# Two transposes taken off TensorE: blocks exchanged by DMA, turned on VectorE

## The chip, the cores and the metric

One core of one Trainium2 chip. The metric is the device time of one execution in microseconds (us), the median of several runs. The kernel before takes 2883.35 us (4 runs, 2882.38 to 2884.21).

## The reference

128 samples of 128 tokens by 512 features, all fp32. Each sample goes through two layers that share one 128x128 adjacency matrix; samples do not depend on each other.

```python
# x: (128, 128, 512), adj: (128, 128); layernorm without affine part, eps 1e-5
h = maximum(layernorm(x), 0)                       # layer 0: graph convolution
x = x + einsum('nm,bmd->bnd', adj, h) @ weight + bias
h = maximum(layernorm(x), 0)                       # layer 1: masked attention, 8 heads of 64
q, k, v = split(h @ w_qkv)
a = softmax(where(adj == 0, -inf, q @ k.T * 64**-0.5))
o = (a @ v) @ w_proj + b_proj
x = x + o + layernorm(o) * ln_gamma + ln_beta
```

## The kernel before

It is a software pipeline over the samples: one turn of the loop works on one sample in each of some twenty stages, and several samples are under way at once. The order of the calls in the loop is the order in which each engine gets its instructions, and the traces show each engine working in that order.

Two operands are transposed before TensorE uses them; as the kernel calls these products, both operands have the axis summed over on the partitions: the normed layer-1 input `h1` (tokens by features becomes features by tokens), and the attention probabilities (8 heads of 128x128). Before, TensorE does it by products with an identity matrix (0.43 and 0.87 us a sample, from the starts in its timeline), and ScalarE copies the results out of PSUM, where the kernel puts them (an evacuation; one of 585 ns and two of 592 ns a sample, medians of L172 and L232).

```python
def norm1_out(i):
    H1[i] = work.tile([P, D], F32, name="h1")
    relu_norm(H1[i], X1[i], *ST1.pop(i))                      # VectorE: shift; ScalarE: relu
    nc.gpsimd.tensor_tensor(X1[i], X1[i], beta_b, op=ALU.add)

def flip(i):                                                   # h1 -> h1T
    ...
    p = mm_psum("pflip")
    for c in range(C):
        nc.tensor.transpose(p[:, c * P:(c + 1) * P], H1[i][:, c * P:(c + 1) * P], ident)
    nc.scalar.copy(H1T[g][:, :, j, :], p.rearrange("p (c n) -> p c n", c=C))
    ...
def softmax_divide(i):
    ...
    nc.gpsimd.tensor_tensor(s, s, sm.unsqueeze(2).to_broadcast([P, H, P]), op=ALU.mult)

def flip_probs(i):                                             # probabilities -> pT
    PT[i] = work.tile([P, 2 * C, P], F32, name="pT")
    for e in range(2):
        p = psum.tile([P, C, P], F32, tag="at", name=f"pp{e}")
        for c in range(C):
            nc.tensor.transpose(p[:, c, :], S[i][:, e * C + c, :], ident)
        nc.scalar.copy(PT[i][:, e * C:(e + 1) * C, :], p)
    ...
for i in range(2 - LOAD, B + 1):
    at(load, i + LOAD - 1)            # nc.sync.dma_start, one DMA of 256 KB (conditions of the first turns cut)
    at(scores, i)
    at(norm1_out, i + 8)
    at(softmax_shift, i)
    at(qk, i + G, 0)
    at(flip_probs, i - 1)
    at(softmax_exp, i)
    at(norm0, i + 11)
    at(qk, i + G, 1)
    at(softmax_divide, i)
    at(norm0_out, i + 11)
    at(attend, i - 1)
    at(values, i + 4)
    at(mix, i + 10)
    at(project, i - 1)
    at(flip, i + 8)
    at(finish, i - 1)                 # ends with nc.sync.dma_start of the result, 256 KB
    at(layer0, i + 9)
```

Only two DMAs a sample leave from the sync queue (SP): the load and the store.

Of the kernel before, what the change touches and what calls it, by code (L numbers as in the profile page):

```python
# [8 lines left out]
F32 = mybir.dt.float32  # L9
AF = mybir.ActivationFunctionType  # L10
ALU = mybir.AluOpType
AX = mybir.AxisListType

P = 128
# [5 lines left out]
def kernel(  # L20
# [22 lines left out]



    nc = tc.nc
    B, N, D = x.shape
    H = 8
    HD = D // H
    C = D // P  # L50
    G = 4
    assert N == P and HD * 2 == P and B % G == 0
    scale = HD ** -0.5

    const = ctx.enter_context(tc.tile_pool(name="const", bufs=1))
    work = ctx.enter_context(tc.tile_pool(name="work", bufs=2))
    stat = ctx.enter_context(tc.tile_pool(name="stat", bufs=4))
    psum = ctx.enter_context(tc.tile_pool(name="psum", bufs=4, space=bass.MemoryType.PSUM))
    ctx.enter_context(tc.manual_schedule())

    X, H0, YT, X1, H1, H1T, QKT, V, S, PT, OT, O, ST0, ST1, STO = ({} for _ in range(15))

    def mm_psum(name):
        return psum.tile([P, 512], F32, tag="mm", name=name)

    def load(i):
        X[i] = work.tile([P, D], F32, name="x", bufs=6)
        nc.sync.dma_start(out=X[i], in_=x[i])

    LOAD = 14  # L70
    for i in range(2):
        load(i)


    ident = const.tile([P, P], F32)
# [16 lines left out]
    def load_layer1():  # L92
        nc.sync.dma_start(out=wqkv_sb, in_=w_qkv.rearrange("(c p) o -> p c o", p=P))
        nc.sync.dma_start(out=wp_sb, in_=w_proj.rearrange("(c p) o -> p c o", p=P))
        for t, src in ((bp_b, b_proj), (gamma_b, gamma), (beta_b, beta)):
            nc.sync.dma_start(out=t, in_=src.partition_broadcast(P))
# [18 lines left out]
    def stats_of(src):  # L115

        st = stat.tile([P, nc.vector.BN_STATS_DIM], F32, name="st")
        nc.vector.bn_stats(st, src)  # L118
        mv = stat.tile([P, nc.vector.BN_AGGR_DIM], F32, name="mv")
        nc.vector.bn_aggr(mv, st)  # L120
        ve = stat.tile([P, 1], F32, name="ve")
        nc.vector.tensor_scalar(ve, mv[:, 1:2], EPS, None, op0=ALU.add)  # L122
        rs = stat.tile([P, 1], F32, name="rs")
        nc.gpsimd.tensor_tensor(rs, ve, minus_half, op=ALU.pow)  # L124
        return mv[:, 0:1], rs

    def relu_norm(dst, src, mean, rs):
        shift = stat.tile([P, 1], F32, name="shift")
        nc.vector.tensor_scalar(shift, mean, rs, -1.0, op0=ALU.mult, op1=ALU.mult)  # L129
        nc.scalar.activation(dst, src, AF.Relu, bias=shift, scale=rs)  # L130
# [6 lines left out]
    def norm0_out(i):  # L137
        relu_norm(H0[i], X[i], *ST0.pop(i))
        nc.gpsimd.tensor_tensor(X[i], X[i], b0_b, op=ALU.add)
# [10 lines left out]
    def layer0(i):  # L150
        p = mm_psum("pl0")
        for c in range(C):
            nc.tensor.matmul(p, lhsT=YT[i][:, c, :], rhs=w0_sb[:, c, :], start=(c == 0), stop=(c == C - 1))  # L153
        X1[i] = work.tile([P, D], F32, name="x1", bufs=12)
        nc.vector.tensor_tensor(X1[i], p, X[i], op=ALU.add)
        ST1[i] = stats_of(X1[i])
        del X[i], YT[i]

    def norm1_out(i):
        H1[i] = work.tile([P, D], F32, name="h1")  # L160
        relu_norm(H1[i], X1[i], *ST1.pop(i))
        nc.gpsimd.tensor_tensor(X1[i], X1[i], beta_b, op=ALU.add)  # L162


    def flip(i):
        g, j = divmod(i, G)
        if j == 0:
            H1T[g] = work.tile([P, C, G, P], F32, name="h1T")
        p = mm_psum("pflip")
        for c in range(C):  # L170
            nc.tensor.transpose(p[:, c * P:(c + 1) * P], H1[i][:, c * P:(c + 1) * P], ident)  # L171
        nc.scalar.copy(H1T[g][:, :, j, :], p.rearrange("p (c n) -> p c n", c=C))  # L172
        del H1[i]

    def qk(i, k):

        g, m = i // G, 2 * (i % G) + k
        if m == 0:
            QKT[g] = work.tile([P, 2 * C, G, P], F32, name="qkT")
        p = mm_psum("pqk")  # L180
# [6 lines left out]
    def values(i):  # L187
        g, j = divmod(i, G)
        p = mm_psum("pv")
        for c in range(C):  # L190
            nc.tensor.matmul(p, lhsT=H1T[g][:, c, j, :], rhs=wqkv_sb[:, c, 2 * D:], start=(c == 0),  # L191
                             stop=(c == C - 1))
        V[i] = work.tile([P, D], F32, name="v", bufs=7)
        nc.scalar.copy(V[i], p)

    def scores(i):

        g, j = divmod(i, G)
        ps = [psum.tile([P, C, P], F32, tag="at", name=f"ps{e}") for e in range(2)]
        for c in range(C):  # L200
            for e in range(2):
                r = slice(e * HD, (e + 1) * HD)
                nc.tensor.matmul(ps[e][:, c, :], lhsT=QKT[g][r, c, j, :], rhs=QKT[g][r, C + c, j, :],  # L203
                                 start=True, stop=True)
        s = S[i] = work.tile([P, 2 * C, P], F32, name="s")
        m4 = maskb.unsqueeze(1).to_broadcast([P, C, P])
        for e in range(2):
            nc.vector.tensor_tensor(s[:, e * C:(e + 1) * C, :], ps[e], m4, op=ALU.add)
# [10 lines left out]
    def softmax_divide(i):  # L219
        s = S[i]  # L220
        sm = stat.tile([P, H], F32, name="sm")
        nc.vector.tensor_reduce(sm, s, AX.X, ALU.add)  # L222
        nc.vector.reciprocal(sm, sm)
        nc.gpsimd.tensor_tensor(s, s, sm.unsqueeze(2).to_broadcast([P, H, P]), op=ALU.mult)  # L224

    def flip_probs(i):
        PT[i] = work.tile([P, 2 * C, P], F32, name="pT")
        for e in range(2):
            p = psum.tile([P, C, P], F32, tag="at", name=f"pp{e}")
            for c in range(C):  # L230
                nc.tensor.transpose(p[:, c, :], S[i][:, e * C + c, :], ident)  # L231
            nc.scalar.copy(PT[i][:, e * C:(e + 1) * C, :], p)  # L232
        del S[i]

    def attend(i):
        p = psum.tile([P, C, P], F32, tag="at", name="po")
# [18 lines left out]
    def finish(i):  # L255
        o = O.pop(i)
        mean, rs = STO.pop(i)
        t = work.tile([P, D], F32, name="t", bufs=3)
        nc.vector.scalar_tensor_tensor(t, o, mean, gamma_b, op0=ALU.subtract, op1=ALU.mult)  # L259
        nc.gpsimd.tensor_tensor(o, o, X1[i], op=ALU.add)  # L260
        nc.vector.scalar_tensor_tensor(t, t, rs, o, op0=ALU.mult, op1=ALU.add)  # L261
        nc.sync.dma_start(out=out[i], in_=t)
        del X1[i]

    def at(f, i, *a):
        if 0 <= i < B:
            f(i, *a)



    for i in range(2 - LOAD, B + 1):
        if i > 2 - LOAD:
            at(load, i + LOAD - 1)
        if i == 4 - LOAD:
            load_layer1()
        at(scores, i)
        at(norm1_out, i + 8)
        at(softmax_shift, i)
        at(qk, i + G, 0)
        at(flip_probs, i - 1)  # L280
        at(softmax_exp, i)
        at(norm0, i + 11)
        at(qk, i + G, 1)
        at(softmax_divide, i)
        at(norm0_out, i + 11)
        at(attend, i - 1)
        at(values, i + 4)
        at(mix, i + 10)
        at(project, i - 1)
        at(flip, i + 8)  # L290
        at(finish, i - 1)
        at(layer0, i + 9)

# [28 lines left out]
```

## Time and profile before

| | before |
|---|---|
| median, us | 2883.35 |
| TensorE (PE) busy | 98% of the span, 97% of the chain that ended last |
| mean steady period of one sample, us | 21.89 |
| DMAs a sample on the sync queue | 2 |
| time that the sync queue waited for data to store | 2643.6 us |

The mean period is taken from the first and the last evacuation of the attention output (`oT`) between 200 and 2500 us, divided by the samples between them; the same rule is used for every kernel. The last row of the table is this one, from the waits of the sync queue of the kernel before (who waited, for what, us in total, times, longest):

```profile
SPq L262 <- DVE t L261: 2643.6, 128, 38.1
```

### The profile page before, as it was taken

What the parts mean: (1) busy time and instruction counts of PE and PEld (TensorE: products, weight loads), DVE (VectorE), ACT (ScalarE), POOL (GpSimd) and SP (SyncE); (2) the same over time, 40 slices, a digit from 0 to 9 for tenths busy, and PEclk for the clock granted to TensorE, in tenths of its full rate; (3) what the DMA queues carried; (4) which work ended last, traced back from release to release, by engine and by line L of the source; (5) the groups of instructions that cost most, each with busy time, mean ns of one, the idle gap of its engine ahead of it and who ended that gap; (6) DMA issues with size and microseconds to landing.
All of it is one profiled execution on the core that took longest, in us unless ns stands there. A gap on an engine that the chain in (4) does not pass through costs nothing.

```text
span 2880.8 us, 30548 instructions
## 1 busy us (share of the span) xinstructions
PE 2825.2 (98%) x11777; PEld 1465.4 (51%) x11777; DVE 1498.2 (52%) x2695; ACT 886.5 (31%) x1410; POOL 992.0 (34%) x902
## 2 busy tenths in 40 slices
PE   7999999999999999999999999999999999999995
PEld 3555555555555555555555555555555555555543
DVE  3355545555554555555455555555545555554544
ACT  2332332333333233233323323332332333233221
POOL 3233333333333333333333333333333333333222
PEclk9999999999999999999999999999999999999997
DMA  3000000000000000000000000000000000000000
GB/s 132 12 22 30 23 23 23 30 23 22 30 23 22 24 28 22 23 30 23 22 26 26 22 22 30 22 23 30 23 23 23 30 23 23 28 25 15 15 15 18
DMA packets 39313, 75.42 MB, mean 26 GB/s; under 512 B 4224, under 2 KB 4352, under 8 KB 39168
## 3 DMA queue, kind: packets, MB, share of 16 engines
q1 hardware_dynamic: 39168, 73.48, 7.9%
q8 instruction: 92, 1.51, 0.2%
q14 instruction: 53, 0.43, 0.1%
HBM read 39.91 MB, written 33.55 MB: 26 GB/s over the span
## 4 chain that ended last, share of the span: by engine, by line
PE 97%; DVE 1%; POOL 0%; issue 0%; ACT 0%; DMA 0%; POOLq 0%; SPq 0%; ACTq 0%
PE pqk L182 31%; PE pv L191 16%; PE pp L249 16%; PE pl L153 15%; PE ps L203 5%; PE po L240 4%; PE pmix L144 4%; PE pp L231 4%; PE pflip L171 2%; DVE st L118 0%; POOL rs L124 0%; POOL o L260 0%; DVE s L214 0%; ACT h L130 0%; DVE mx L213 0%
## 5 line engine op out<-in xcount | busy, mean ns | idle before, releaser
L182 PE MATMUL pqk<-h1T,wqkv_sb 128*128 128x512 f32 x2048 | 933.1, 599 | 0.0
L124 POOL TENSOR_TENSOR rs<-ve,minus_half 128x1 f32<-128x1 f32 x384 | 258.6, 674 | 1462.6 <-DVE ve L122 1462.2
L251 DVE TENSOR_TENSOR o<-pp,bp_b 128x512 f32<-128x512 f32 x128 | 88.5, 692 | 1003.5 <-PE pp L249 1003.5
L182 PEld LDWEIGHTS pqk<-h1T,wqkv_sb 128*128 128x128 f32 x2048 | 369.3, 190 | 386.7 <-issue 371.6
L130 ACT ACTIVATE h<-x,shift,rs 128x512 f32<-128x512 f32 x256 | 208.4, 814 | 951.2 <-DVE shift L129 951.2
L249 PE MATMUL pp<-wp_sb,oT 128*128 128x512 f32 x1024 | 472.5, 605 | 26.1 <-ACT oT L243 26.1
L191 PE MATMUL pv<-wqkv_sb,h1T 128*128 128x512 f32 x1024 | 473.1, 605 | 0.0
L153 PE MATMUL pl<-w_sb,yT 128*128 128x512 f32 x1024 | 466.5, 599 | 0.0
L224 POOL TENSOR_TENSOR s<-s,sm 128x1024 f32<-128x1024 f32 x128 | 242.7, 1896 | 194.2 <-DVE shift L129 124.3
L249 PEld LDWEIGHTS pp<-wp_sb,oT 128*128 128x128 f32 x1024 | 189.4, 195 | 220.5 <-issue 193.2
L191 PEld LDWEIGHTS pv<-wqkv_sb,h1T 128*128 128x128 f32 x1024 | 184.4, 189 | 207.2 <-issue 207.2
L153 PEld LDWEIGHTS pl<-w_sb,yT 128*128 128x128 f32 x1024 | 186.8, 192 | 187.5 <-issue 187.5
L214 DVE TENSOR_TENSOR s<-s,mx 128x1024 f32<-128x1024 f32 x128 | 257.0, 2008 | 4.4
L162 POOL TENSOR_TENSOR x<-x,beta_b 128x512 f32<-128x512 f32 x128 | 176.2, 1376 | 208.4 <-ACT h L130 204.3
L261 DVE SCALAR_TENSOR_TENSOR t<-t,rs,o 128x512 f32<-128x512 f32 x128 | 96.2, 751 | 213.8 <-POOL o L260 213.8
L172 ACT COPY h1T<-pflip 128x512 f32<-128x512 f32 x128 | 74.9, 585 | 384.8 <-PE pflip L171 384.8
L185 ACT COPY qkT<-pqk 128x512 f32<-128x512 f32 x256 | 147.3, 575 | 114.3 <-PE pqk L182 114.3
L118 DVE BATCH_NORM_STATS2 st<-x 128x6 f32<-128x512 f32 x256 | 176.2, 688 | 5.1 <-DMA x<-in_x_dram 0.7
L217 ACT ACTIVATE s<-s 128x1024 f32<-128x1024 f32 x128 | 135.6, 1059 | 140.0 <-DVE s L214 140.0
L203 PEld LDWEIGHTS ps<-qkT 64*128 64x128 f32 x2048 | 124.2, 187 | 96.7 <-issue 96.7
L222 DVE TENSOR_REDUCE sm<-s 128x8 f32<-128x1024 f32 x128 | 156.2, 1220 | 27.7 <-ACT s L217 15.8
L144 PEld LDWEIGHTS pmix<-adjT,h 128*128 128x128 f32 x1024 | 135.8, 194 | 65.7 <-issue 59.6
(40 smaller groups left out, 2411.0 us busy)
## 6 DMA issues: line engine op xcount, KB each, us to landing
x<-in_x_dram SPq DMA_DIRECT2D x128, 256.0 KB, 2.7
out_dram<-t SPq DMA_DIRECT2D x128, 256.0 KB, 2.0
wqkv_sb<-in_L_gnn_w_qkv_dram SPq DMA_DIRECT2D x1, 3072.0 KB, 15.3
w_sb<-in_L_gnn_weight_dram SPq DMA_DIRECT2D x1, 1024.0 KB, 7.9
wp_sb<-in_L_gnn_w_proj_dram SPq DMA_DIRECT2D x1, 1024.0 KB, 17.5
b_b<-in_L_gnn_bias_dram SPq DMA_DIRECT2D x1, 256.0 KB, 5.4
bp_b<-in_L_gnn_b_proj_dram SPq DMA_DIRECT2D x1, 256.0 KB, 16.2
gamma_b<-in_L_gnn_ln_gamma_dram SPq DMA_DIRECT2D x1, 256.0 KB, 14.8
```

The source lines that it names most:

```text
L118: nc.vector.bn_stats(st, src)
L124: nc.gpsimd.tensor_tensor(rs, ve, minus_half, op=ALU.pow)
L130: nc.scalar.activation(dst, src, AF.Relu, bias=shift, scale=rs)
L144: nc.tensor.matmul(p[:, c * P:(c + 1) * P], lhsT=H0[i][:, c * P:(c + 1) * P], rhs=adjT, start=True, stop=True)
L153: nc.tensor.matmul(p, lhsT=YT[i][:, c, :], rhs=w0_sb[:, c, :], start=(c == 0), stop=(c == C - 1))
L162: nc.gpsimd.tensor_tensor(X1[i], X1[i], beta_b, op=ALU.add)
L182: nc.tensor.matmul(p, lhsT=wqkv_sb[:, c, m * P:(m + 1) * P], rhs=H1T[g][:, c, :, :].rearrange("p b n -> p (b n)"), start=(c == 0), stop=(c ...
L191: nc.tensor.matmul(p, lhsT=H1T[g][:, c, j, :], rhs=wqkv_sb[:, c, 2 * D:], start=(c == 0), stop=(c == C - 1))
L203: nc.tensor.matmul(ps[e][:, c, :], lhsT=QKT[g][r, c, j, :], rhs=QKT[g][r, C + c, j, :], start=True, stop=True)
L214: nc.vector.tensor_tensor(s, s, mx.unsqueeze(2).to_broadcast([P, H, P]), op=ALU.subtract)
L224: nc.gpsimd.tensor_tensor(s, s, sm.unsqueeze(2).to_broadcast([P, H, P]), op=ALU.mult)
L249: nc.tensor.matmul(p, lhsT=OT[i][:, c, :], rhs=wp_sb[:, c, :], start=(c == 0), stop=(c == C - 1))
```

## The change

The intent is to take both transposes off TensorE. A 128x128 transpose is cut in 32x32 blocks. Sixteen DMAs, all between on-chip tiles, bring block (n, q) to the place of block (q, n); one VectorE instruction then turns each block in itself (0.71 us for `h1`, 1.24 us for the probabilities in the run after, whose result is correct). Two such exchanges a sample make 32 DMAs on the sync queue, beside the load and the store.

```diff
-        X[i] = work.tile([P, D], F32, name="x", bufs=6)
+        X[i] = work.tile([P, D], F32, name="x", bufs=5)
...
+    def exchange(dst, src):
+        for n in range(Q):                                   # Q, R = 4, 32
+            for q in range(Q):
+                nc.sync.dma_start(out=dst[q * R:(q + 1) * R, n, :], in_=src[n * R:(n + 1) * R, q, :])
...  (norm1_out)
-        H1[i] = work.tile([P, D], F32, name="h1")
-        relu_norm(H1[i], X1[i], *ST1.pop(i))
+        h1 = work.tile([P, Q, C, R], F32, name="h1")
+        relu_norm(h1.rearrange("p q c r -> p c q r"), X1[i].rearrange("p (c q r) -> p c q r", c=C, q=Q),
+                  *ST1.pop(i))
+        H1[i] = work.tile([P, Q, C * R], F32, name="h1x")
+        exchange(H1[i], h1.rearrange("p q c r -> p q (c r)"))
...  (flip)
-        p = mm_psum("pflip")
-        for c in range(C):
-            nc.tensor.transpose(p[:, c * P:(c + 1) * P], H1[i][:, c * P:(c + 1) * P], ident)
-        nc.scalar.copy(H1T[g][:, :, j, :], p.rearrange("p (c n) -> p c n", c=C))
+        nc.vector.transpose(H1T[g][:, :, j, :].rearrange("p c (q r) -> p q c r", q=Q),
+                            H1.pop(i).rearrange("p q (c r) -> p q c r", c=C))
...  (softmax_divide)
-        nc.gpsimd.tensor_tensor(s, s, sm.unsqueeze(2).to_broadcast([P, H, P]), op=ALU.mult)
+        sq = work.tile([P, Q, H, R], F32, name="sq", bufs=1)
+        nc.gpsimd.tensor_tensor(sq, s.rearrange("p h (q r) -> p q h r", q=Q),
+                                sm.unsqueeze(1).unsqueeze(3).to_broadcast([P, Q, H, R]), op=ALU.mult)
+        S[i] = work.tile([P, Q, H * R], F32, name="sx")
+        exchange(S[i], sq.rearrange("p q h r -> p q (h r)"))
...  (flip_probs)
-        for e in range(2):
-            ...                                              # 4 transposes and one copy each
+        nc.vector.transpose(PT[i].rearrange("p h (q r) -> p q h r", q=Q),
+                            S.pop(i).rearrange("p q (h r) -> p q h r", h=H))
...  (loop)
     for i in range(2 - LOAD, B + 1):
+        at(norm1_out, i + 8)
...
-        at(norm1_out, i + 8)
...
-        at(qk, i + G, 1)
+        at(mix, i + 10)
         at(softmax_divide, i)
         at(norm0_out, i + 11)
+        at(qk, i + G, 1)
         at(attend, i - 1)
         at(values, i + 4)
-        at(mix, i + 10)
+        at(flip, i + 8)
         at(project, i - 1)
-        at(flip, i + 8)
         at(finish, i - 1)
```

Cut: smaller buffer counts for `x1`, `s` and `t`, which make room for the new tiles.

More of the change, by code (lines that the diff above doesn't have):

```diff
@@ L51 @@
     G = 4
+    Q, R = 4, 32
     assert N == P and HD * 2 == P and B % G == 0
@@ L153, in layer0 @@
             nc.tensor.matmul(p, lhsT=YT[i][:, c, :], rhs=w0_sb[:, c, :], start=(c == 0), stop=(c == C - 1))
-        X1[i] = work.tile([P, D], F32, name="x1", bufs=12)
+        X1[i] = work.tile([P, D], F32, name="x1", bufs=11)
         nc.vector.tensor_tensor(X1[i], p, X[i], op=ALU.add)
@@ L168, in flip @@
             H1T[g] = work.tile([P, C, G, P], F32, name="h1T")
-        p = mm_psum("pflip")
-        for c in range(C):
-            nc.tensor.transpose(p[:, c * P:(c + 1) * P], H1[i][:, c * P:(c + 1) * P], ident)
-        nc.scalar.copy(H1T[g][:, :, j, :], p.rearrange("p (c n) -> p c n", c=C))
-        del H1[i]
+        nc.vector.transpose(H1T[g][:, :, j, :].rearrange("p c (q r) -> p q c r", q=Q),
+                            H1.pop(i).rearrange("p q (c r) -> p q c r", c=C))
     def qk(i, k):
@@ L204, in scores @@
                                  start=True, stop=True)
-        s = S[i] = work.tile([P, 2 * C, P], F32, name="s")
+        s = S[i] = work.tile([P, 2 * C, P], F32, name="s", bufs=1)
         m4 = maskb.unsqueeze(1).to_broadcast([P, C, P])
@@ L223, in softmax_divide @@
         nc.vector.reciprocal(sm, sm)
-        nc.gpsimd.tensor_tensor(s, s, sm.unsqueeze(2).to_broadcast([P, H, P]), op=ALU.mult)
+        sq = work.tile([P, Q, H, R], F32, name="sq", bufs=1)
[3 more added lines that the diff above has]
+        exchange(S[i], sq.rearrange("p q h r -> p q (h r)"))
     def flip_probs(i):
         PT[i] = work.tile([P, 2 * C, P], F32, name="pT")
-        for e in range(2):
-            p = psum.tile([P, C, P], F32, tag="at", name=f"pp{e}")
-            for c in range(C):
-                nc.tensor.transpose(p[:, c, :], S[i][:, e * C + c, :], ident)
-            nc.scalar.copy(PT[i][:, e * C:(e + 1) * C, :], p)
-        del S[i]
+        nc.vector.transpose(PT[i].rearrange("p h (q r) -> p q h r", q=Q),
+                            S.pop(i).rearrange("p q (h r) -> p q h r", h=H))
     def attend(i):
@@ L257, in finish @@
         mean, rs = STO.pop(i)
-        t = work.tile([P, D], F32, name="t", bufs=3)
+        t = work.tile([P, D], F32, name="t", bufs=2)
         nc.vector.scalar_tensor_tensor(t, o, mean, gamma_b, op0=ALU.subtract, op1=ALU.mult)
```

## The prediction

> **What bounds the kernel now.** I read the page's busy shares first, then the chain that ended last, then the groups of instructions with shapes kept apart, and last the timeline of single engines in one steady period.
>
> Busy shares and chain, from the page:
> ```profile
> PE 2825.2 (98%) x11777; PEld 1465.4 (51%) x11777; DVE 1498.2 (52%) x2695; ACT 886.5 (31%) x1410; POOL 992.0 (34%) x902
> PE 97%; DVE 1%; POOL 0%; issue 0%; ACT 0%; DMA 0%; POOLq 0%; SPq 0%; ACTq 0%
> PE pqk L182 31%; PE pv L191 16%; PE pp L249 16%; PE pl L153 15%; PE ps L203 5%; PE po L240 4%; PE pmix L144 4%; PE pp L231 4%; PE pflip L171 2%; DVE st L118 0%; POOL rs L124 0%; POOL o L260 0%; DVE s L214 0%; ACT h L130 0%; DVE mx L213 0%
> ```
> TensorE is the bound, 97% of the chain. The lines to be removed are the transposes, L231 (4%) and L171 (2%).
>
> One steady period on TensorE, from its timeline (start, duration, instruction):
> ```profile
> 2008.74 0.60 PE L171 MATMUL pflip<-ident,h 128*128 128x128 f32 x4
> 2009.17 3.60 PE L153 MATMUL pl<-w_sb,yT 128*128 128x512 f32 x8
> 2012.70 1.16 PE L203 MATMUL ps<-qkT 64*128 64x128 f32 x16
> 2013.79 3.70 PE L182 MATMUL pqk<-h1T,wqkv_sb 128*128 128x512 f32 x8
> 2017.33 1.04 PE L231 MATMUL pp<-ident,s 128*128 128x128 f32 x8
> 2018.20 3.60 PE L182 MATMUL pqk<-h1T,wqkv_sb 128*128 128x512 f32 x8
> 2021.73 1.09 PE L240 MATMUL po<-pT,v 128*64 128x128 f32 x16
> ...
> 2030.62 0.60 PE L171 MATMUL pflip<-ident,h 128*128 128x128 f32 x4
> ```
> From start to start there is no gap: the period is 2030.62 - 2008.74 = 21.88 us a sample. Ends overlap, so I cost by differences of starts: pflip takes 9.17 - 8.74 = 0.43 us, the eight probability transposes 18.20 - 17.33 = 0.87 us.
>
> VectorE in the same period:
> ```profile
> 2008.94 0.69 DVE L251 TENSOR_TENSOR o<-pp,bp_b 128x512 f32<-128x512 f32 x1 [7.93 <-PE pp L249]
> ...
> 2015.42 0.15 DVE L122 TENSOR_SCALAR ve<-mv 128x1 f32<-128x1 f32 x1
> 2015.50 1.28 DVE L208 TENSOR_TENSOR s<-ps,maskb 128x512 f32<-128x512 f32 x2
> 2016.69 0.20 DVE L129 TENSOR_SCALAR shift<-mv,rs 128x1 f32<-128x1 f32 x1
> 2016.81 1.22 DVE L213 TENSOR_REDUCE mx<-s 128x8 f32<-128x1024 f32 x1
> 2018.06 2.17 DVE L214 TENSOR_TENSOR s<-s,mx 128x1024 f32<-128x1024 f32 x1
> ```
> VectorE waits 7.93 us for the projection and then works without much pause until after the softmax. That the engine is 52% busy hides that its work lies in one burst right after the projection; a thing added to the burst can reach TensorE.
>
> DMA issue, from the queue's timeline and the DMA view:
> ```profile
> 1.65 0.42 SPq L81 DMA_DIRECT2D adj_sb<-in_adj_dram  x1
> 2.12 0.43 SPq L83 DMA_DIRECT2D b_b<-in_L_gnn_bias_dram  x1
> 2.59 0.43 SPq L85 DMA_DIRECT2D w_sb<-in_L_gnn_weight_dram  x1
> out_dram<-t SPq DMA_DIRECT2D x128, 256.0 KB, 2.0
> ```
> A free queue issues one DMA per 0.47 us whether it holds 64 KB or 1 MB; 256 KB lands 2.0 us after issue.
>
> [...] The trace before has no such instruction. [...] For N=1024 [...] the undisturbed row L213 of that size shows 1.22 us, so I use the row for the transpose. [...] L214 takes 2.17 us beside GpSimd's addition of beta and 1.22 us in other periods.
>
> **The change part by part, per sample.**
> Removed: 12 TensorE transposes, 0.43 + 0.87 = 1.30 us of pure bound, and three ScalarE evictions of about 0.59 us, off the path. TensorE alone could then run at 21.88 - 1.30 = 20.58 us.
> Added on the queue: 32 DMAs. With load and store 34 x 0.47 = 16.0 us of 20.6: busy 78%, but it fits. Each DMA waits for the semaphore of the one eight before it, so it is held only if landing takes over 8 x 0.47 = 3.8 us; I expect 2. The queue is in order, so I lay it out from t = 0 at L251's start: h1 is ready about 8.6, its 16 DMAs end at 16.1, the load at 16.6; the divided probabilities are ready about 17.2, their 16 DMAs end at 24.7 and land near 26.7, and the store (25.7) follows. They are needed in the next period, at 11.3 + 20.8 = 32. h1 lands about 18, its transpose (0.7 us) ends before VectorE's next projection work at 20.8. Both are hidden with 2 to 5 us to spare. It would stop to fit near 0.6 us a DMA.
> Added on VectorE: one transpose of 1024 elements, 1.22 us, and one of 512, 0.69 us as L251. Busy is then (1498 + 128 x 1.91)/128 = 13.6 us a sample, far from the period, but the place counts. Moved: the shift of layer 1's norm now comes ahead of the mask addition, and so waits for GpSimd's power (0.55 us). In the burst: ve ends at 6.63, power at 7.35, shift at 7.6, two mask additions to 8.8, maximum to 10.05, subtraction to 11.3 (1.22, for GpSimd's addition of beta should be over at 9.9), transpose to 12.5, semaphore 0.1: probabilities ready at 12.6. TensorE wants them at 21.73 - 8.94 - 0.43 = 12.36 (the mix of 0.89 us has taken the place of the 0.87 us of transposes). So TensorE waits some 0.25 us, and the period is about 20.8 us: 1.07 us saved.
> Over the 120 or so full periods: 128 us saved.
> At the start: until the first q/k product, layers run one sample after the other, at 40.90 us minus 31.40 us = 9.5 us in one step. With VectorE blocked by the exchange a step is addition and statistics 1.8, power, shift and relu 2.0, issue 7.5, landing 2, transpose 0.8: 14 us. Four such steps: 20 us lost. At the end TensorE is cold and waiting already; each of the last five samples gets the transpose in its chain (some 2 us), the last one also an exchange that nothing hides (7 us), and four before them lose about 1: some 22 us lost.
> Sum: 2883 - 128 + 42 = 2797 us.
>
> **The rivals.** (a) TensorE stays the only bound, all 1.30 us are kept and the ends cost little: 2883 - 157 + 30 = 2756 us. For it: 97% of the chain. Against: VectorE's burst worked out above is already at the edge. (b) VectorE's chain becomes the bound: if eight semaphore waits ahead of a transpose, or a disturbed subtraction (2.17 us), add 0.5 to 0.9 us, the period is 21.3 to 21.7 and the time 2850 to 2900, the gain lost. [...] (c) The queue becomes the bound: at 0.65 us per DMA, or with landing over 5 us, 34 x 0.65 = 22 us a period and 2980. For it: during the load of the weights issues took 1.9 us each; against: those queued behind 3 MB, while the exchanges move 16 or 32 KB each and the DMA engines are now at 8%.
>
> **Range and chances.** I take 2797 as the middle; (a) gives the lower edge, 2755, and the milder half of (b) the upper, 2855. Faster by 2% means under 2826: that holds unless the burst costs more than 0.25 us beyond my count. Faster 0.70, within 2% 0.23, slower 0.07 (the queue, or a slow transpose).
>
> **What would show it.** Right: a period of 20.6 to 21.0 us in TensorE's timeline; before L248 (attention times values) short waits for the VectorE transpose; transposes of about 1.2 and 0.7 us; queue issues of 0.4 to 0.5 us; first q/k product near 73 us instead of 54. Wrong: the queue issuing without a pause, VectorE's transposes waiting on DMA in the steady state, transposes of 2 us or more, or TensorE waits before L248 of over 0.5 us a sample.

What no trace or run of this case shows is cut above, each cut marked: in the paragraph before "The change part by part", of which only what the trace's own rows say remains ("no such instruction" there means a transpose on VectorE), and in (b) the case of 2930 us for a slower transpose. The 1.22 us of the transpose is the estimate from the row of L213 (median 1217 ns before).

Measured, to be read beside it: in the trace before, all 106 subtractions (L214) of over 1.8 us overlap GpSimd's addition of beta; of the 22 others, of 1.22 to 1.23 us, 8 overlap none, and in 14 the addition started 0.1 us after the subtraction and itself took 2.24 to 2.27 us, where its median is 1.27. What a DMA waits for is in the operands of that trace: 256 of the 264 DMAs of the sync queue wait for the semaphore of the one eight before, all but the first eight. The eight semaphores ahead of a transpose are in the trace after: in all 256 transposes, seven in four instructions ahead of it (21 to 50 ns each when nothing is waited for, some 0.1 us apart), one on the transpose. And what the prediction calls cold: in the last 61 us TensorE was busy for 33.2 us at a granted clock of 0.70, after 1.00 from 54 to 2780 us.

## The result, and the profile after

**2955.68 us** (4 runs, 2952.68 to 2958.98), correct. The ratio to before is 1.0251 (95% interval 1.0233 to 1.0269): slower by 2.5%, where 3% faster was predicted. Ratios in this document are the mean time of one kernel's fast runs over the mean of the other's fast runs of the same rounds, so they are not quite the ratio of the medians quoted.

The page of the kernel after, busy shares and then the chain that ended last:

```profile
PE 2688.3 (91%) x10241; PEld 1320.5 (45%) x10241; DVE 1630.4 (55%) x2951; ACT 666.4 (23%) x1026; POOL 989.3 (34%) x902
SPq 67%; DVE 12%; issue 8%; POOL 5%; PE 4%; DMA 3%; ACT 1%; DVEq 0%; POOLq 0%; ACTq 0%
```

TensorE did lose 137 us of busy time, and VectorE gained 132 us (its transposes take 249.5 us, while the subtraction of the maximum fell from 257.0 to 156.8 us). But TensorE has gone from the chain. In its place stands SPq, the sequencer of the sync queue. The engines' busy shares cannot show this: issuing a DMA does not count as busy.

The timeline of the sync queue in the kernel after (start, duration, instructions joined):

```profile
1998.95 0.53 SPq L270 DMA_DIRECT2D out_dram<-t  x1
1999.57 10.46 SPq L133 DMA_DIRECT2D h1x<-h  x16
2010.13 0.53 SPq L70 DMA_DIRECT2D x<-in_x_dram  x1
2010.76 10.02 SPq L133 DMA_DIRECT2D sx<-sq  x16
2020.87 0.53 SPq L270 DMA_DIRECT2D out_dram<-t  x1
```

From one store to the next pass 2020.87 - 1998.95 = 21.92 us, and each row starts about 0.1 us after the one before it ends. The queue never rests: 34 issues fill a whole period. Its waits for the result to store have shrunk from 2643.6 us to

```profile
SPq L270 <- DVE t L269: 18.4, 4, 15.8
```

What one issue takes is in the view of the issuing line, between 1000 and 2000 us (shortest/median/longest in ns):

```profile
L133 SPq DMA_DIRECT2D sx<-sq x734: 507/588/1710, 999.6 to 1998.3; - x184
```

The median is 588 ns, and 0.04 us pass between two issues, which makes 0.63 us; with the few that are stretched to over 1 us the mean over the period is 21.98 / 34 = 0.646 us. This division takes the queue to be full, and the trace bears it out: between 200 and 2500 us issues fill 91.6% of the time, the rest is short gaps between them, and those of over 0.2 us make up only 0.5%. Nor does the sync queue wait for landings: the one such wait in its list is of 1.4 us, at the very end. In this trace too a DMA waits for the one eight before it (4352 of 4360, all but the first eight), but that costs nothing here: a landing takes 1.8 to 1.9 us, eight issues 8 x 0.63 = 5.0.

How a full queue delays TensorE can be seen on GpSimd, VectorE and TensorE of the kernel after, in the same stretch. GpSimd divides the probabilities:

```profile
2004.98 1.91 POOL L233 TENSOR_TENSOR sq<-s,sm 128x1024 f32<-128x1024 f32 x1 [0.89 <-DVE shift L137]
```

They are ready at 2006.89, and their exchange starts at 2010.76: they stand in the queue for 3.9 us. VectorE:

```profile
2011.55 0.71 DVE L180 STREAM_TRANSPOSE h1T<-h1x 128x512 f32<-128x512 f32 x1 [6.71 <-DMA h1x<-h]
2012.19 0.65 DVE L259 TENSOR_TENSOR o<-pp,bp_b 128x512 f32<-128x512 f32 x1
...
2023.37 1.24 DVE L240 STREAM_TRANSPOSE pT<-sx 128x1024 f32<-128x1024 f32 x1
```

TensorE:

```profile
2002.47 1.09 PE L248 MATMUL po<-pT,v 128*64 128x128 f32 x16 [0.78 <-DVE pT L240]
...
2007.04 3.60 PE L257 MATMUL pp<-wp_sb,oT 128*128 128x512 f32 x8
...
2024.66 1.09 PE L248 MATMUL po<-pT,v 128*64 128x128 f32 x16 [1.54 <-DVE pT L240]
```

VectorE reaches the transpose of h1 early and waits 6.71 us for the exchange. In VectorE's order the addition of the projection's bias (L259) stands behind it: the projection ended at 2007.04 + 3.60 = 2010.64, and L259 starts at 2012.19, 1.55 us late. The burst behind it then runs its 12.42 us (2012.19 to the end of the transpose at 2024.61), and TensorE waits 1.54 us for it before `po`. So the wait that TensorE shows names VectorE, while the cause is two steps back on the sync queue.

### The profile page after: what moved, and what is told of

Read it like the earlier page. It is cut to its first block, busy times and chain, and to the rows that moved or that the text cites. A ratio compares the mean times of both kernels' runs of the same rounds, so it can differ in the third digit from the quotient of the medians.

```text
span 2952.6 us, 32999 instructions
## 1 busy us (share of the span) xinstructions
PE 2688.3 (91%) x10241; PEld 1320.5 (45%) x10241; DVE 1630.4 (55%) x2951; ACT 666.4 (23%) x1026; POOL 989.3 (34%) x902
## 4 chain that ended last, share of the span: by engine, by line
SPq 67%; DVE 12%; issue 8%; POOL 5%; PE 4%; DMA 3%; ACT 1%; DVEq 0%; POOLq 0%; ACTq 0%
SPq L133 64%; DMA h1x<-h 3%; POOL rs L126 3%; DVE st L120 2%; POOL o L268 2%; DVE s L216 2%; SPq L270 2%; PE pp L257 2%; SPq L70 1%; PE pv L199 1%; DVE t L269 1%; DVE h1T L180 1%; DVE x L163 1%; DVE o L259 1%; DVE mx L221 1%
## 5 line engine op out<-in xcount | busy, mean ns | idle before, releaser
L190 PE MATMUL pqk<-h1T,wqkv_sb 128*128 128x512 f32 x2048 | 937.6, 601 | 22.1 <-issue 18.7
L180 DVE STREAM_TRANSPOSE h1T<-h1x 128x512 f32<-128x512 f32 x128 | 91.1, 711 | 852.2 <-DMA h1x<-h 844.9
L199 PE MATMUL pv<-wqkv_sb,h1T 128*128 128x512 f32 x1024 | 486.5, 619 | 0.0
L248 PE MATMUL po<-pT,v 128*64 128x128 f32 x2048 | 146.1, 287 | 199.5 <-DVE pT L240 198.9
L257 PEld LDWEIGHTS pp<-wp_sb,oT 128*128 128x128 f32 x1024 | 197.9, 194 | 255.3 <-issue 204.3
L161 PEld LDWEIGHTS pl<-w_sb,yT 128*128 128x128 f32 x1024 | 196.6, 193 | 246.2 <-issue 246.2
L233 POOL TENSOR_TENSOR sq<-s,sm 128x1024 f32<-128x1024 f32 x128 | 244.5, 1910 | 175.9 <-DVE sm L231 67.4
L248 PEld LDWEIGHTS po<-pT,v 128*64 128x64 f32 x2048 | 114.0, 141 | 302.6 <-DVE pT L240 242.9
L173 POOL TENSOR_TENSOR x<-x,beta_b 128x512 f32<-128x512 f32 x128 | 162.2, 1268 | 150.7 <-ACT h L138 149.2
L147 POOL TENSOR_TENSOR x<-x,b_b 128x512 f32<-128x512 f32 x128 | 162.4, 1269 | 16.5 <-ACT h L138 16.5
L216 DVE TENSOR_TENSOR s<-ps,maskb 128x512 f32<-128x512 f32 x256 | 163.5, 680 | 0.0
## 6 DMA issues: line engine op xcount, KB each, us to landing
wqkv_sb<-in_L_gnn_w_qkv_dram SPq DMA_DIRECT2D x1, 3072.0 KB, 15.6
```

The lines of the kernel that those rows point to most:

```text
L147: nc.gpsimd.tensor_tensor(X[i], X[i], b0_b, op=ALU.add)
L161: nc.tensor.matmul(p, lhsT=YT[i][:, c, :], rhs=w0_sb[:, c, :], start=(c == 0), stop=(c == C - 1))
L190: nc.tensor.matmul(p, lhsT=wqkv_sb[:, c, m * P:(m + 1) * P], rhs=H1T[g][:, c, :, :].rearrange("p b n -> p (b n)"), start=(c == 0), stop=(c ...
L199: nc.tensor.matmul(p, lhsT=H1T[g][:, c, j, :], rhs=wqkv_sb[:, c, 2 * D:], start=(c == 0), stop=(c == C - 1))
L216: nc.vector.tensor_tensor(s[:, e * C:(e + 1) * C, :], ps[e], m4, op=ALU.add)
L233: nc.gpsimd.tensor_tensor(sq, s.rearrange("p h (q r) -> p q h r", q=Q), sm.unsqueeze(1).unsqueeze(3).to_broadcast([P, Q, H, R]), op=ALU.mult)
```

## The experiments

The theory ("queue"): the period is the number of issues on the sync queue times 0.646 us. The rivals: "burst", VectorE's chain from L259 to the transpose is too long; and "data", the traffic of many small pieces is slow to land, whoever issues it. All runs of a batch shared the runs of the kernel before: 2882.55 us for e1 to e4, 2881.29 us for e5 to e8 (7 runs each).

| run | issues a sample on the sync queue | median us | ratio to before (95%) | mean period us | first q/k product, us |
|---|---|---|---|---|---|
| before | 2 | 2883.35 | | 21.89 | 53.83 |
| after | 34 | 2955.68 | 1.0251 (1.0233 to 1.0269) | 21.98 | 83.84 |
| e1 | 26, and 8 on ScalarE's | 2996.84 | 1.0399 (1.0384 to 1.0415) | 22.55 | 67.33 |
| e2 | 26 | 2774.03 | 0.9626 (0.9611 to 0.9640) | 20.63 | 73.26 |
| e3 | 18 | 2817.17 | 0.9773 (0.9757 to 0.9789) | 21.14 | 55.87 |
| e4 | 10 | 2762.79 (one run) | | 20.70 | 52.34 |
| e5 | 26, and 8 on ScalarE's | 2832.06 | 0.9830 (0.9815 to 0.9845) | 20.99 | 83.42 |
| e6 | 34, all from HBM | 2764.94 (one run) | | 20.70 | 55.83 |
| e7 | 26 | 2732.53 | 0.9483 (0.9467 to 0.9499) | 20.63 | 54.79 |
| e8 | 36 | 3115.24 | 1.0813 (1.0797 to 1.0829) | 23.37 | 83.78 |

All are correct, but for e4 and e6, which compute a wrong result; of those two there is one run each, so only their periods and issue times are used.

### e1: half of h1's exchange issued from ScalarE's queue

```diff
-    def exchange(dst, src):
+    def exchange(dst, src, on_act=0):
-                nc.sync.dma_start(...)
+                (nc.scalar if n < on_act else nc.sync).dma_start(...)
-        exchange(H1[i], h1.rearrange("p q c r -> p q (c r)"))
+        exchange(H1[i], h1.rearrange("p q c r -> p q (c r)"), 2)
```

> Half of the exchange of h1 (8 of 32 DMAs a sample) is issued from ScalarE's queue. Queue theory: the sync queue issues 34 DMAs at 0.63 us and that sets the period of 22.1 us after; with 26 it needs 26 x 0.645 = 16.8 us, falls idle in each sample, and the period goes to what VectorE's burst allows, 20.8 to 21.3 us; time 2780 to 2830 us. Rival, VectorE's burst or the landing of the blocks: the period stays within 0.3 us of 22.1 and the time near 2950.

Measured: 2996.84 us, a miss: it got slower, not faster. ScalarE's timeline in e1:

```profile
2001.96 0.81 ACT L138 ACTIVATE h<-x,shift,rs 128x512 f32<-128x512 f32 x1 [10.93 <-DVE shift L137]
2002.81 5.28 ACTq L133 DMA_DIRECT2D h1x<-h  x8
2008.13 0.58 ACT L193 COPY qkT<-pqk 128x512 f32<-128x512 f32 x1 [5.35 <-DMA h1x<-h]
```

ScalarE's issues stand in one row with its own instructions. Eight of them (median 602 ns there) hold its own instructions up for 5.28 us, among them the copy of a q/k product and, behind that, the exponential that the softmax needs; 19% of e1's chain is now these issues. So e1 does relieve the sync queue, but says nothing of what that is worth: it puts a second cost in the place of the first. For the steady state it does not speak against the queue theory, and does not support it either. Only the start speaks: with half of h1's issues off the sync queue the first q/k product comes at 67.33 us, 16.5 us earlier than in after.

### e2: the blocks on the diagonal copied by engines, not by DMAs

Four of the sixteen blocks stay in their own partitions and need no DMA. ScalarE copies those of h1 (296 ns each), GpSimd those of the probabilities (392 ns each).

```diff
+                if n != q:
                     nc.sync.dma_start(out=dst[q * R:(q + 1) * R, n, :], in_=src[n * R:(n + 1) * R, q, :])
+        for q in range(Q):
+            stay(dst[q * R:(q + 1) * R, q, :], src[q * R:(q + 1) * R, q, :])
...  (stay is nc.scalar.copy for h1, nc.gpsimd.tensor_copy for the probabilities)
```

> The four blocks of each exchange that stay in their quadrant are copied by ScalarE (h1) and GpSimd (probabilities) in place of a DMA; 24 DMAs a sample in place of 32, result still right. Queue theory: 26 issues x 0.645 = 16.8 us, period 20.8 to 21.3 us, time 2780 to 2830. Rival, VectorE's burst: unchanged near 2950, or worse because of four more instructions on two engines.

Measured: 2774.03 us, 3.7% faster than before and 6.1% below after; time and period (20.63 us) lie just below the expected ranges. The sync queue in e2:

```profile
1999.17 8.81 SPq L134 DMA_DIRECT2D sx<-sq  x12
2008.08 0.53 SPq L273 DMA_DIRECT2D out_dram<-t  x1
2011.39 7.47 SPq L134 DMA_DIRECT2D h1x<-h  x12
```

Between the store and the exchange of h1 it rests 2.78 us: it waits for its data again, as its waits over the whole run say:

```profile
SPq L134 <- ACT h L141: 410.7, 127, 9.1
```

TensorE in e2, from one attention product to the next:

```profile
2015.44 1.09 PE L251 MATMUL po<-pT,v 128*64 128x128 f32 x16
...
2036.07 1.09 PE L251 MATMUL po<-pT,v 128*64 128x128 f32 x16
```

2036.07 - 2015.44 = 20.63 us, the period that the prediction gave for TensorE alone (20.58), and no wait is marked. VectorE's burst is the same as in after (from the bias addition at 2003.00 to the end of the transpose at 2015.38: 12.38 us), and no longer in the way. This speaks against the rival "burst": nothing was taken from VectorE. The bytes moved by DMA fell with the issues, so "data" is not excluded by e2.

### e3: the exchange for the probabilities only

h1 goes back to TensorE, with `norm1_out` and `flip` as before.

```diff
-        exchange(H1[i], h1.rearrange("p q c r -> p q (c r)"))
+        H1[i] = work.tile([P, D], F32, name="h1")
+        relu_norm(H1[i], X1[i], *ST1.pop(i))
... and flip() with four TensorE transposes and one ScalarE copy
```

> Only the probabilities go by DMA and VectorE; h1 is transposed on TensorE again. Queue theory: 18 issues x 0.645 = 11.6 us, no bound; TensorE needs 21.88 - 0.87 = 21.0 us, and it asks for the probabilities 0.43 us later than after, so waits little; time 2780 to 2810 (start as before, some 15 us lost at the end). Rival, the place of the probabilities' transpose in VectorE's burst bounds: 2850 or more.

Measured: 2817.17 us, just above the expected range; the period is 21.14 us. TensorE alone would allow 21.89 - 0.87 = 21.02, so with 18 issues (some 11.6 us) nothing but a tenth of a microsecond is lost in the steady state. The start is nearly that of before (55.87 us to the first q/k product): the 30 us that after loses there belong to h1's exchange. The excess over the expectation is at the end: from the 119th evacuation of the attention output to the last instruction the trace of e3 takes 178.5 us, the one of before 158.4, so that 20 us are lost where some 15 were expected.

### e4: four DMAs of 128 partitions each (wrong result)

The same bytes to the same tiles, in 4 pieces instead of 16; no block changes its place, so the result is wrong.

```diff
-        for n in range(Q):
-            for q in range(Q):
-                nc.sync.dma_start(out=dst[q * R:(q + 1) * R, n, :], in_=src[n * R:(n + 1) * R, q, :])
+        for q in range(Q):
+            nc.sync.dma_start(out=dst[:, q, :], in_=src[:, q, :])
```

> Wrong result on purpose: the same bytes go in 4 DMAs of 128 partitions per exchange instead of 16 of 32. It measures the issue: if a copy within the on-chip memory costs 0.59 us whatever its shape, these show 0.59; if the 32-partition shape is what costs, they show 0.43 as the loads at the start do. Queue theory for the time: 10 issues, 5 to 6 us, period 20.8 to 21.3, some 2780 us.

Measured: 2762.79 us with a period of 20.70. Each issue, four times as large, costs what the small ones cost:

```profile
L132 SPq DMA_DIRECT2D sx<-sq x512: 464/593/1881, 125.0 to 2736.0; - x171
```

So with the same bytes the loss is gone; what counts is the number of issues. That speaks against "data" as far as bytes go, though the pieces per DMA differ too.

### e5: half of the probabilities' exchange from ScalarE, late in the loop

As e1, but where ScalarE has nothing urgent: eight of the sixteen issues of the probabilities stand at the end of the loop body.

```diff
-        exchange(S[i], sq.rearrange("p q h r -> p q (h r)"))
+        SQ[i] = sq
+        exchange(S[i], sq.rearrange("p q h r -> p q (h r)"), range(2), nc.sync)
...  (exchange takes the blocks and the queue)
+    def exchange_rest(i):
+        exchange(S[i], SQ.pop(i).rearrange("p q h r -> p q (h r)"), range(2, Q), nc.scalar)
...
         at(layer0, i + 9)
+        at(exchange_rest, i)
```

> Half of the probabilities' exchange (8 DMAs a sample) is issued from ScalarE's queue, at the end of the period where the trace of e1 shows ScalarE waiting 10.9 us. If e1 was slow because its issues stood ahead of the exponential in ScalarE's order, this one is not: sync queue 26 x 0.645 = 16.8 us, period 20.6 to 20.9 as in e2, start as slow as after (16 issues in each step); time 2780 to 2800 us. If issuing from two queues at once is itself slow: period 22 or more, time above 2930.

Measured: 2832.06 us, 1.7% faster than before, but above the expected 2780 to 2800. The slow start (first q/k product at 83.42 us, as in after) had been expected; what was missed is the period, 20.99 us where 20.6 to 20.9 were expected. 16 issues of h1 still stand in one row; VectorE in e5:

```profile
2007.99 0.71 DVE L182 STREAM_TRANSPOSE h1T<-h1x 128x512 f32<-128x512 f32 x1 [5.09 <-DMA h1x<-h]
2008.72 0.69 DVE L265 TENSOR_TENSOR o<-pp,bp_b 128x512 f32<-128x512 f32 x1
```

The transpose of h1 ends just when the bias addition starts, so nothing is left over for a stretched issue, and the mean period is 20.99 us though the period in this stretch is 20.69. In the trace the lost time comes in single periods: 42 of 109 are longer than 20.8 us, and the period after a row of h1 of more than 10.5 us (10.0 is the usual length) takes 21.41 us on average (25 cases). In e2, with 12 issues, the transpose ends at 2000.45 and the addition starts at 2003.00: 2.55 us to spare. Relief of the queue's total is needed, and so is relief of the longest row of issues that something waits for.

### e6: the same 32 DMAs, read from HBM (wrong result)

```diff
-                nc.sync.dma_start(out=dst[q * R:(q + 1) * R, n, :], in_=src[n * R:(n + 1) * R, q, :])
+                nc.sync.dma_start(out=dst[q * R:(q + 1) * R, n, :], in_=x[i][n * R:(n + 1) * R, q * W:q * W + src.shape[2]])
...  (W, a column step that keeps the reads inside x[i], and the argument i)
```

> Wrong result on purpose: the same 32 DMAs with the same shapes and order, but they read x in HBM, not the tile on chip. If reading on-chip memory is what makes an issue 0.59 us (the loads at the start took 0.43), the median here is 0.43 to 0.45 and the period falls to about 20.7 us (34 x 0.48 = 16.3 us), time near 2780. If it is the rate of DMAs issued back to back, the median stays at 0.59 and the time near 2950.

Measured: 2764.94 us, period 20.70. As many issues and as many bytes, to the same places, but from HBM:

```profile
L134 SPq DMA_DIRECT2D h1x<-in_x_dram x2048: 310/419/2233, 14.8 to 2583.6; - x187
```

An issue takes 419 ns instead of 588; 34 x (0.42 + 0.04) = 15.6 us fit, as the prediction had reckoned. One caution: these DMAs do not wait for h1 or the probabilities, so the run also lacks that dependence, which is why its start is not delayed. It shows the cost of an issue, and that the queue with 34 cheaper issues does not bind; it is no version to keep.

### e7: e2, with TensorE transposes where nothing hides the exchange

Both ends of the run lose by the exchange, since there a sample runs alone (in e2 the first q/k product comes 19.4 us later than before, and the stretch from the 119th evacuation of the attention output to the end takes 178.3 us in place of 158.4). e7 takes TensorE for h1 of the first 4 samples and for the probabilities of the last 9, and e2's form for all others.

```diff
+    LAST = B - 9
...
+        if i < G:        # norm1_out and flip as in the kernel before
...
+        if i >= LAST:    # softmax_divide and flip_probs as in the kernel before
```

> e2 with TensorE transposing again where TensorE has time: h1 of the first four samples, probabilities of the last nine. Steady period unchanged at 20.63. Start as before, first q/k product near 54 us in place of 73 in e2: 19 us less. End: periods of 17 us in place of 19 and no bare exchange: some 12 us less. 2774 - 31 = 2743 us, range 2735 to 2760.

Measured: 2732.53 us, correct, 5.2% faster than before and just below the expected range: the best version here. TensorE is the chain again:

```profile
PE 96%; DVE 2%; POOL 1%; issue 0%; ACT 0%; DMA 0%; POOLq 0%; SPq 0%; DVEq 0%; ACTq 0%
```

### e8: two issues more

To the kernel after, load and store are each cut into two DMAs of 64 partitions: the same bytes, 36 issues instead of 34, nothing else.

```diff
-        nc.sync.dma_start(out=X[i], in_=x[i])
+        for a in range(2):
+            nc.sync.dma_start(out=X[i][a * 64:(a + 1) * 64], in_=x[i][a * 64:(a + 1) * 64])
... and the store alike
```

> The change as it is, with load and store of a sample each cut in two DMAs of 64 partitions: 36 issues in place of 34, same bytes, right result. Queue theory: each costs 0.63 us, period 21.98 + 1.26 = 23.2 us, 128 periods: 160 us more, 3090 to 3125. Rival (landing, VectorE's burst): no change, 2945 to 2965.

Measured: 3115.24 us, 160 us above after. The period rises by 23.37 - 21.98 = 1.39 us; 36 issues at the 0.646 us of after would take 23.26 us. The sync queue in e8:

```profile
2008.32 1.19 SPq L71 DMA_DIRECT2D x<-in_x_dram  x2
...
2019.74 1.18 SPq L272 DMA_DIRECT2D out_dram<-t  x2
```

Two where one took 0.53 us: 0.66 and 0.65 us more, with the gaps some 1.4 us. Neither "burst" nor "data" gives 1.4 us a sample for two issues without a byte more. The granted clock of TensorE was lower in this run (0.953, after 0.977, before 0.990), while its busy share was 89%; since it waits even so (1.54 us before `po` in the period shown by its timeline, for VectorE's transpose, as in after), that does not explain the 1.39 us, which the queue's own timeline accounts for.

### e9: the cost of an issue by itself

Nine rows of six DMAs each at the start of the kernel before: three sources by three numbers of partitions. Only the durations of these issues are read.

```diff
+    for k in range(6):
+        nc.sync.dma_start(out=probe[0:32, k, :], in_=x[k][0:32, 0:P])      # from HBM
...
+    for k in range(6):
+        nc.sync.dma_start(out=probe[0:32, k, :], in_=xs[32:64, k, :])      # from on-chip memory
... and with 64 and 128 partitions, and with contiguous rows of HBM
```

> The kernel before with nine bursts of six small DMAs ahead of everything else, result right, time some 25 to 40 us longer: only the issue durations are looked at. Bursts: HBM rows in strided form to 128, 64, 32 partitions; HBM contiguous to 128, 64, 32; on-chip to on-chip, 128, 64, 32 partitions. If both ends on chip is what costs: 0.42 in the first six bursts, 0.59 in the last three, whatever the partitions. If it is partitions below 128: 0.42 for 128 and 0.59 for 64 and 32 in all three kinds; e6 (0.42 for 32 from HBM) and e8 (0.59 for 64 from HBM) cannot both fit either, so I expect a contiguous source of few partitions to be slow as well.

Measured, from the views of four of the nine lines (64 and 32 partitions from HBM, 128 and 32 from on-chip memory):

```profile
L77 SPq DMA_DIRECT2D probe<-in_x_dram x6: 562/596/602, 3.5 to 6.7; - x6
L79 SPq DMA_DIRECT2D probe<-in_x_dram x6: 417/420/582, 7.3 to 9.8; - x6
L87 SPq DMA_DIRECT2D probe<-xs x6: 518/599/603, 19.9 to 23.0; - x6
L91 SPq DMA_DIRECT2D probe<-xs x6: 588/589/592, 27.5 to 30.7; - x6
```

Medians in ns:

| source | 128 partitions | 64 | 32 |
|---|---|---|---|
| HBM, strided rows | 432 | 596 | 420 |
| HBM, contiguous rows | 430 | 594 | 420 |
| on-chip memory | 599 | 595 | 589 |

From on-chip memory to on-chip memory an issue costs 0.59 to 0.60 us in all three shapes; from HBM 0.42 to 0.43, except for 64 partitions (0.59 to 0.60). Whether the rows in HBM are contiguous makes 2 ns at most. Why 64 partitions should be dear, and why two on-chip ends add some 0.17 us, no run here shows. All these are issues in a row; the first of a row can differ (518 ns in the row of 128 partitions from on-chip memory, whose others take 599 to 603).

## Why the prediction was wrong, step by step

**The step that failed** is the one on the queue: "34 x 0.47 = 16.0 us of 20.6: busy 78%, but it fits". The 0.47 came from three issues that read HBM at the start of the run, and was carried over to DMAs between two on-chip tiles, of which the kernel before has none. Those take 0.588 us, 0.646 us all in: 34 of them fill 21.98 us, against the 20.6 that TensorE would need. The prediction named the edge ("It would stop to fit near 0.6 us a DMA") and had the outcome as rival (c), at 0.65 us a DMA, but gave it and a slow transpose together a chance of 0.07. (The 2980 us of (c) do not follow from its own terms: 120 periods of 22.1 us and the 42 us of the ends give some 2951.) Nothing in the trace before measured an issue between two on-chip tiles, and so the one number on which everything rested was not in evidence. Shown by e8 (two issues added: +1.39 us), e2 (eight taken away: the period falls to TensorE's own), e4 and e6 (fewer issues, or cheaper ones, with as many bytes to the tiles: no loss) and e9 (the cost by itself).

Source and destination are not all that counts. The store is the same DMA in both kernels; the views of its line, before and then after:

```profile
L262 SPq DMA_DIRECT2D out_dram<-t x128: 332/343/347, 153.6 to 2878.0; - x128
L270 SPq DMA_DIRECT2D out_dram<-t x128: 338/526/536, 195.9 to 2949.8; - x128
```

It takes 0.34 us on the idle queue of before and 0.53 us directly behind an exchange; the load's median goes from 0.38 to 0.53 us. In after the first issue of an exchange, behind a load or a store, takes 0.507 us, each further one 0.588 us. So no single figure of the trace before, its 0.47 included, could be carried over to a full queue of other DMAs.

**The layout on the queue** fails as its consequence. It left 4.6 us free in a period. In fact the probabilities stand 3.9 us in the queue, and VectorE's transpose of h1 waits 6.71 us and pushes the bias addition 1.55 us back.

**TensorE's own limit** was right: 20.58 us predicted, 20.63 in e2 and e7.

**VectorE's transposes** were right: 1237 and 711 ns, predicted 1.22 and 0.69 us. (An estimate from these two: 526 ns for 512 elements more, 1.03 ns an element, and some 0.18 us besides.) The subtraction of the maximum takes 1.22 us in every sample of after, as reckoned: no GpSimd instruction runs beside it there, while before 106 of 128 took over 1.8 us (median 2.17), each beside GpSimd's addition of beta. The burst was right too: 12.4 us in after and in e2, predicted 12.6. The wait of 0.25 us expected before the attention product does not appear in e2, where no wait is marked. Rival (b) is thereby refuted for this kernel.

**The landing time** was right: 1.8 and 1.9 us, predicted 2. Only the issues in front of it were mis-sized. With 0.63 us from one issue to the next some three DMAs were under way at a time (an estimate: 1.9 / 0.63).

**The start** was mis-sized for the same reason. The first q/k product comes 30.0 us later than before, predicted 20: sixteen issues took 10.0 us in each of the steps, not 7.5. In e2, with twelve (7.5 us), it comes 19.4 us later.

**The end** was right: in the traces, the stretch from the 119th evacuation of the attention output to the last instruction takes 158.4 us before and 181.7 us after, 23.3 more (predicted 22); in e2 it takes 178.3 us. Up to the sixth evacuation, after takes 39.4 us more than before, so the start costs some 9 us more than its first q/k product shows. With 9.1 us from the periods between, these parts make up the 71.8 us by which the span grew. In e7, which mends both ends, the last stretch takes 157.6 us, and -148.8 us stand against -120 x 1.26 = -151.

So the gain of 1.3 us a sample on TensorE was real. It was given back in the steady state to a queue that had been idle, and the ends made it a loss. With eight issues fewer the gain comes back whole, and with the ends mended it is 149 us.

**What stays open**: why the issue between two on-chip tiles is dearer; why an issue directly behind such a one is dearer too; why 64 partitions from HBM cost as much; and why single issues are stretched to 1.0 to 1.9 us (up to 1.7 us in the row shown of after), which lifts the mean from 0.63 to 0.646.

## What to carry to other kernels

In this kernel the sync queue had a throughput of its own (34 issues in 21.98 us). So count the issues in a period and multiply by the measured time of an issue *of the same source and destination, in a row of its like* (here 0.42 us from HBM to 32 partitions and 0.59 us between on-chip tiles); if the kernel at hand has no such issue, measure one before you build on it. The busy shares of the page do not count issuing (in after TensorE's 91% was the largest, while SPq was 67% of the chain), so look at the queue's own timeline and waits: a queue that waits for data has time to spare (2643.6 us before); one in which, over a whole period, each issue starts at the end of the last (within 0.1 us in after) can be the bound, even where the trace names another engine, and one or two issues more will show it (+1.39 us a sample in e8). Issues moved to ScalarE's queue stopped ScalarE for as long as they lasted (5.28 us a sample in e1), so first take away the pieces that need no DMA (here the blocks on the diagonal: 3.7% faster than before in e2), and leave the ends of the run, where nothing hides a latency, to the old way (5.2% in e7).
